# Cross-attention and a spectral feed-forward layer on one core: the rows of W are no longer folded, the first matrix sum runs for even and odd rows apart, and the first six tiles are reordered

## The chip, the cores and the metric

The kernel runs on one core of one Trainium2 chip. The metric is the time of one execution on the device in microseconds (us); lower is better. Five engines work side by side, each through its own list of instructions in order, and wait for each other by semaphores: TensorE (PE, with its weight loads shown apart as PEld), VectorE (DVE), ScalarE (ACT), GpSimd (POOL) and SyncE (SP), which here only issues transfers. PE writes to PSUM, a small memory of banks; DVE or ACT copies results from there to SBUF.

## The reference

Two blocks follow each other on x, of shape (2, 2048, 512), all in float32. The first is cross-attention with 16 heads of 32 over 128 context rows. The second is a linear layer given by its spectrum W, a complex 512 x 512 matrix.

```
x = x + attention(layernorm(x), ctx, mask)
    q = h @ wq + bq;  k = ctx @ wk + bk;  v = ctx @ wv + bv
    score = (q . k) / sqrt(32) * mask;  score = -1e9 where score == 0
    softmax(score) @ v, heads joined, @ wo + bo
x = x + real(ifft(fft(layernorm(x)) @ W)) + bias
```

The second block is linear, so the kernel computes one real 512 x 512 matrix from W and the tables of cosines and sines, and multiplies with that.

## The kernel before

The 4096 rows of x are cut into 8 groups of 512, and each group into 4 tiles of 128 rows. A tile is written (group, tile) here: (0,0), (0,1) and so on. A tile begins with its score products: `scores` (L309) makes 16 heads in two halves of eight, each half in a PSUM buffer of its own (`ps_sc`, two buffers, so one tile at a time). For each half `Softmax` does:

- `masked` (L338, DVE): product with the mask, which frees the score buffer
- `maxima` (L345, L347, L348, DVE): the marking of zeros, the smallest negated score and its scaling
- `exponentials` (L354, ACT): eight exponentials, each with its sum
- `divided` (L366 on DVE, L367 on POOL): the reciprocal of the sums and the product with it

`transposed_weights` (L384) transposes the finished weights of the tile before on PE, a PSUM bank for four heads, and copies each bank out on ACT or DVE. It runs in two halves of two banks. `context` (L406) multiplies with v when all four tiles of a group are there, `Project` makes the output product o (L204), `Ffn` the second block's product y (L204), and `Queries` the queries (L204), whose copy with the bias is on ACT (L297). Rows of x are prepared two groups ahead: `relative` (L238) subtracts the first element of each row, `query_statistics` (DVE, then rstd on POOL, L217 and L218) finds mean and deviation, `query_norm` (L221, DVE) applies them and `query_transposes` (L190, copied by ACT on L192) turns a tile.

Three PSUM pools decide what PE may start: `ps_sc`, `ps_tp` with two banks for transposes, and `ps_mm` with two banks for everything else. A product waits until the copy from the bank two products earlier has ended.

**How the matrix m_ffn is made.** W's real and imaginary parts, `wr` and `wi`, have the symmetry of rows k and 512 - k under cosine and sine. `FoldRows` (L606) uses it: a matmul with the flipped identity `flip` turns a block of rows, and DVE writes the sum and the difference of the two blocks (L625, L628), with the row 0 put in by hand (L627, L630). `fold_columns` (L636, POOL) does the same for columns and writes `cols`. Then the first sum, four `Mirrored` objects `h`, multiplies `cols` by half of the tables (`dft`, 256 rows): columns 0 to 256 by cosines, 1 to 255 by sines, two matmuls each (L689). The eviction (L697) copies the cosine half with an added first row and the sine half, and writes cosine minus sine, mirrored, and cosine plus sine. The result is `half`. The second sum, four `Mirrored` objects `m`, does the same with `half` and writes `m_ffn`. The added rows come over small transfers (`rows_h`, `rows_m`, L667) and a small transpose on PE (L673).

**What sets the order.** All instructions are placed by hand. The first five tiles, (0,0) to (1,0), are written out (L847 to L970) and hold the preparation of m_ffn between their softmax steps. From (1,1) on, `slot` (L724) lays out a tile in a fixed scheme: scores, then `pool` and `early` work, the first maximum, a first product, the first exponentials, the second mask product and so on. With its argument `soon` the first exponentials stand ahead of the first product's copy and DVE copies the first two transposed banks; the second exponentials then stand ahead of ACT's copies of the last two. Before, one tile (6,1) is laid out so. The loop at L973 calls `slot` for groups 1 to 5; tile (1,2) begins with the transposes of group 3 (L1016). The last two groups are written out again.

SP issues all loads of x, masks, weights and tables and most stores, in program order. A load into a buffer that is still read waits on that queue, and everything behind it too. `wr` and `wi` lie in the two buffers that later hold the residual rows `x_0` and `x_1`.

Of the kernel before, what the change touches and what calls it, by code (L numbers as in the profile page):

```python
# [9 lines left out]
FP = mybir.dt.float32  # L10
# [4 lines left out]
P = 128  # L15
# [7 lines left out]
def kernel(  # L23
# [76 lines left out]
    flip = const_tile([P, P], "flip")  # L100
    nc.vector.tensor_copy(flip, ident[:, P - 1 :: -1])
# [55 lines left out]

    wr = big_tile("x", 2, "wr")
    wi = big_tile("x", 2, "wi")
    row0 = const_tile([1, 2, D], "row0")  # L160
    nc.sync.dma_start(row0[:, 0, :], wf_re[0:1, :])
    nc.sync.dma_start(row0[:, 1, :], wf_im[0:1, :])
    nc.sync.dma_start(wr[:, :HC, :], chunks(wf_re[1 : HD + 1, :]))
    nc.sync.dma_start(wr[:, HC:, :], chunks(wf_re[HD:, :]))
    nc.sync.dma_start(wi[:, :HC, :], chunks(wf_im[1 : HD + 1, :]))
    nc.sync.dma_start(wi[:, HC:, :], chunks(wf_im[HD:, :]))
# [4 lines left out]
    nc.sync.dma_start(dft[:, :HC, :], chunks(dft_cos[HD:, :]))  # L171
    nc.sync.dma_start(dft[:, HC:, :], chunks(dft_sin[HD:, :]))
# [27 lines left out]
    def chain(name, lhs, rhs, width=D, between=()):  # L200

        ps = ps_mm.tile([P, D], FP, tag="mm", name=name)[:, :width]
        for c in range(NC):
            nc.tensor.matmul(  # L204
                ps, lhs(c), rhs(c), start=(c == 0), stop=(c == NC - 1)
            )
            if c == HC - 1:
                call(between)
        return ps
# [69 lines left out]
    class Queries:  # L279


        def __init__(self, i, g, first=0):
            self.i, self.g, self.first = i, g, first

        def pe(self):
            i, g = self.i, self.g
            if i not in qTs:
# [5 lines left out]
                width=GQ - self.first * P,  # L293
            )

        def evict(self):
            nc.scalar.activation(  # L297
                qTs[self.i][:, self.g, self.first * P :],
                self.ps,
                AF.Identity,  # L300
                bias=bq[:, self.g : self.g + 1],
            )
# [299 lines left out]
    m_ffn = const_tile([P, NC, D], "m_ffn")  # L602
    half = big_tile("pt", 6, "half")
    cols = big.tile([P, 4, HC, HD], FP, tag="cT", bufs=1, name="cols")

    class FoldRows:  # L606
# [3 lines left out]
        def __init__(self, name, t, other, sign, c):  # L610
            self.name, self.t, self.other, self.sign = name, t, other, sign
            self.c = c

        def pe(self):

            t, c = self.t, self.c
            self.low = ps_mm.tile([P, D], FP, tag="mm", name=f"low_{self.name}_{c}")
            nc.tensor.matmul(
                self.low, flip, t[:, HC - 1 - c, :], start=True, stop=True
            )  # L620

        def evict(self):
            t, c = self.t, self.c
            total, high = t[:, HC - 1 - c, :], t[:, HC + c, :]
            nc.vector.tensor_tensor(total, self.low, high, ALU.add)  # L625
            if c == 0:
                nc.vector.tensor_copy(total[0:1, :], high[0:1, :])  # L627
            nc.vector.tensor_tensor(high, high, self.low, ALU.subtract)  # L628
            if c == 0:
                nc.vector.tensor_scalar(  # L630
                    high[0:1, :], row0[:, self.other, :], self.sign, None, ALU.mult
                )

        on_vector = True

    def fold_columns():  # L636


        up, down = slice(HD + 1, D), slice(HD - 1, 0, -1)
        rp, rm, ip, im = wr[:, :HC, :], wr[:, HC:, :], wi[:, :HC, :], wi[:, HC:, :]  # L640
        for k, (x1, x2, op, first) in enumerate(
            (
                (rp[:, :, up], rp[:, :, down], ALU.add, rp[:, :, HD : HD + 1]),
                (im[:, :, up], im[:, :, down], ALU.add, im[:, :, HD : HD + 1]),
                (ip[:, :, down], ip[:, :, up], ALU.subtract, rp[:, :, 0:1]),
                (rm[:, :, up], rm[:, :, down], ALU.subtract, im[:, :, 0:1]),
            )
        ):
            nc.gpsimd.tensor_tensor(cols[:, k, :, 1:], x1, x2, op)
            nc.gpsimd.tensor_copy(cols[:, k, :, 0:1], first)  # L650

    def cols_of(what, g):
        return lambda i: cols[
            :,
            2 * what + i // HC,
            HC - 1 - i if i < HC else i - HC,
            g * P : (g + 1) * P,
        ]
# [11 lines left out]
    def first_rows(name, rows, scale):  # L670
# [4 lines left out]
        nc.scalar.mul(add, ps, scale)  # L675
        return add

    class Mirrored:
# [3 lines left out]
        def __init__(self, name, lhs, dst, scale):  # L682
            self.name, self.lhs, self.dst, self.scale = name, lhs, dst, scale

        def pe(self):
            ps = ps_mm.tile([P, D], FP, tag="mm", name=self.name)
            self.even, self.odd = ps[:, : HD + 1], ps[:, HD + 1 :]
            for i in range(NC):
# [3 lines left out]
                    dft[:, i, : HD + 1] if i < HC else dft[:, i, 1:HD],  # L692
# [4 lines left out]
        def evict(self, add, eng=nc.gpsimd):  # L697
            low, high = self.dst[:, 1:HD], self.dst[:, D - 1 : HD : -1]
            nc.scalar.activation(
                self.dst[:, : HD + 1],  # L700
                self.even,
                AF.Identity,
                bias=add,
                scale=self.scale,
# [117 lines left out]
    for t in range(TG):  # L822
        relative(1, t, nc.gpsimd if t < 2 else nc.vector)
    query_statistics(1, 0, TG - 1)
    for g in range(NC):
        first_queries(0, g)
# [406 lines left out]
```

## Time and profile before

| what | us |
|---|---|
| median of 3 runs | 538.68 (538.62 to 538.73) |
| profiled execution, its own time | 538.3 |
| its span, from the first to the last instruction | 536.1 |
| PE idle until the ident of POOL is there (L523) | 1.3 |
| PE idle before y, waiting for x (L507) | 0.6 |
| PE idle before the second pair of turned tiles, waiting for xnT (L192), two times | 0.5 |
| first score product, tile (0,0), starts | 20.1 |
| score product of (1,0) starts | 80.8 |
| score product of (1,2) starts | 112.0 |
| four tiles in the middle, (2,0) at 141.47 to (3,0) at 202.06 | 60.6 |

The span is some 2 us shorter than the time of the same execution. Busy time of PE counts each matmul with its latency, so neighbouring matmuls overlap in it; the distance between the starts of two products tells more than the sum of their lengths. The granted clock of TensorE was 0.999 over the span. Each matmul in float32 shows as two instructions in the trace, here called passes, each with its weight load.

### The profile page before, as it was taken

The page shows a single profiled execution, that of the slowest core. Times are in us where ns is not written, and L with a number is a line of the kernel's source. Part 1 is how long each engine was busy: PE and PEld are TensorE (multiplying, and loading weights), DVE is VectorE, ACT ScalarE, POOL GpSimd, SP SyncE. Part 2 cuts the span into 40 slices and gives each one's busy share as a digit, 9 for nine tenths or more (in the row PEclk, how much of TensorE's full clock was granted, in tenths as well). Part 3 has the DMA queues.
Part 4 walks back from the last instruction along what each step waited for, and adds up shares of the span by engine and source line. Part 5 has one row for each costly group of instructions (what it writes and reads, how often), then busy time and mean ns, then how long its engine had stood idle before and what let it go on. Part 6 is the DMA issues. An engine that isn't in the chain of part 4 may idle for free.

```text
span 536.1 us, 8773 instructions
## 1 busy us (share of the span) xinstructions
PE 525.3 (98%) x3005; PEld 293.2 (55%) x3005; DVE 439.4 (82%) x619; ACT 342.2 (64%) x1299; POOL 326.5 (61%) x266
## 2 busy tenths in 40 slices
PE   8979999999999999999999999999999999999997
PEld 7745567455545555455545555455545555455444
DVE  4698887799987998879887998879967899898351
ACT  3376786676687766666677666666776676766210
POOL 3246768935795449825795459825754466856450
PEclk9999999999999999999999999999999999999999
DMA  8960203000510005000510006000311201201102
GB/s 310 384 228 1 70 10 100 1 0 2 190 47 2 20 28 209 1 21 1 192 45 0 21 20 205 13 20 1 119 40 31 70 1 60 98 2 39 40 0 79
DMA packets 22992, 36.49 MB, mean 68 GB/s; under 512 B 2202, under 2 KB 6562, under 8 KB 22948
## 3 DMA queue, kind: packets, MB, share of 16 engines
q1 hardware_dynamic: 22260, 34.75, 18.7%
q10 hardware_dynamic: 688, 1.18, 0.6%
q8 instruction: 24, 0.39, 0.3%
q14 instruction: 20, 0.16, 0.1%
HBM read 27.53 MB, written 8.39 MB: 67 GB/s over the span
## 4 chain that ended last, share of the span: by engine, by line
PE 76%; DVE 17%; ACT 5%; POOL 1%; issue 1%; ACTq 0%; POOLq 0%; DVEq 0%
PE y L204 16%; PE o L204 16%; PE q L204 15%; PE tpw L384 8%; PE c L406 5%; PE sc L319 5%; ACT w L354 4%; DVE w L345 4%; DVE nmax L347 3%; DVE w L338 3%; PE tp_a L190 3%; PE tp_f L190 2%; PE k L551 1%; PE v L204 1%; DVE norm_f L221 1%
## 5 line engine op out<-in xcount | busy, mean ns | idle before, releaser
L354 ACT ACTIVATE w<-w,nmax 128x128 f32<-128x128 f32 x512 | 198.3, 395 | 19.6 <-DVE nmax L348 18.0
L367 POOL TENSOR_TENSOR w<-w,rden 128x1024 f32<-128x1024 f32 x62 | 119.3, 1924 | 83.4 <-DVE rden L366 67.2
L204 PE MATMUL o<-wo,cT 128*128 128x512 f32 x256 | 115.3, 594 | 0.0
L204 PE MATMUL q<-xnT,wq 128*128 128x512 f32 (+1 forms) x256 | 112.0, 582 | 2.6 <-ACT qT L297 1.5
L204 PE MATMUL y<-m_ffn,nT 128*128 128x512 f32 x248 | 112.1, 594 | 0.6 <-DVE x L507 0.6
L391 ACT COPY pt<-tpw 128x512 f32<-128x512 f32 x120 | 64.1, 587 | 56.5 <-PE tpw L384 56.4
L354 ACT ACTIVATION_READ_ACCUMULATOR w<-w,nmax 128x1 f32 x512 | 98.9, 193 | 0.0
L345 DVE SCALAR_TENSOR_TENSOR w<-w 128x1024 f32<-128x1024 f32 x64 | 88.7, 1386 | 0.9
L338 DVE TENSOR_TENSOR w<-sc,mask 128x1024 f32<-128x1024 f32 x64 | 77.4, 1211 | 12.4 <-PE sc L319 11.8
L347 DVE TENSOR_REDUCE nmax<-w 128x8 f32<-128x1024 f32 x64 | 78.1, 1220 | 2.2
L384 PEld LDWEIGHTS tpw<-ident,w 128*128 128x128 f32 x496 | 57.7, 141 | 31.8 <-issue 29.3
L204 PEld LDWEIGHTS q<-xnT,wq 128*128 128x128 f32 x256 | 46.3, 190 | 48.6 <-issue 40.2
L204 PEld LDWEIGHTS o<-wo,cT 128*128 128x128 f32 x256 | 46.2, 190 | 47.5 <-issue 46.1
L204 PEld LDWEIGHTS y<-m_ffn,nT 128*128 128x128 f32 x248 | 44.5, 190 | 45.2 <-issue 44.2
L384 PE MATMUL tpw<-ident,w 128*128 128x128 f32 x496 | 64.8, 273 | 0.7 <-POOL m_ffn L711 0.5
L462 POOL TENSOR_TENSOR x<-x,bf 128x512 f32<-128x512 f32 x32 | 50.5, 1577 | 19.0 <-DVE norm_f L221 19.0
L217 POOL TENSOR_SCALAR rstd_f<-mv_f 128x1 f32<-128x1 f32 x32 | 18.1, 564 | 65.1 <-DVE mv_f L214 65.1
L422 POOL TENSOR_TENSOR x<-x,bo 128x512 f32<-128x512 f32 x32 | 47.9, 1529 | 0.0
L238 POOL TENSOR_SCALAR rel<-rows 128x512 f32<-128x512 f32 x26 | 42.3, 1639 | 1.3 <-PE tp_a L190 1.3
L319 PEld LDWEIGHTS sc<-kT,qT 32*128 32x128 f32 x1024 | 31.5, 186 | 15.1 <-issue 12.9
L366 DVE RECIPROCAL rden<-den 128x8 f32<-128x8 f32 x64 | 12.6, 197 | 32.1 <-ACT w L354 31.9
L192 ACT COPY nT<-tp_f 128x512 f32<-128x512 f32 x29 | 16.9, 582 | 33.8 <-PE tp_f L190 33.6
(100 smaller groups left out, 552.4 us busy)
## 6 DMA issues: line engine op xcount, KB each, us to landing
rows<-in_x_dram SPq DMA_DIRECT2D x32, 256.0 KB, 5.2
x<-in_x_dram SPq DMA_DIRECT2D x32, 256.0 KB, 4.6
out_dram<-x SPq DMA_DIRECT2D x31, 256.0 KB, 2.0
mask<-in_mask_Bx1xSxS_fk_dram SPq DMA_DIRECT2D x8, 256.0 KB, 5.0
wk<-in_L_xattn_wk_w_dram ACTq DMA_DIRECT2D x2, 512.0 KB, 6.3
wq<-in_L_xattn_wq_w_dram SPq DMA_DIRECT2D x1, 1024.0 KB, 7.6
wr<-n_L_ffn_w_freq_real_dram SPq DMA_DIRECT2D x2, 512.0 KB, 5.2
wi<-n_L_ffn_w_freq_imag_dram SPq DMA_DIRECT2D x2, 512.0 KB, 7.4
```

The lines of the kernel that those rows point to most:

```text
L204: nc.tensor.matmul(ps, lhs(c), rhs(c), start=(c == 0), stop=(c == NC - 1))
L238: eng.tensor_scalar(d, xt, xt[:, 0:1], None, ALU.subtract)
L319: nc.tensor.matmul(sc[r // 2][:, r % 2, g, :], qTs[i][rows, g, t * P : (t + 1) * P], kT[rows, g, b * K : (b + 1) * K], start=True, stop=True,)
L338: nc.vector.tensor_tensor(self.w, self.sc.rearrange("p r g k -> p (r g) k"), self.mrow, ALU.mult)
L345: nc.vector.scalar_tensor_tensor(w, w, 0.0, w, ALU.is_equal, ALU.subtract)
L347: nc.vector.tensor_reduce(self.nmax, w, AX.X, ALU.min)
L354: nc.scalar.activation(w[:, h, :], w[:, h, :], AF.Exp, bias=self.nmax[:, h : h + 1], scale=-UNIT, accum_out=self.den[:, h : h + 1],)
L367: eng.tensor_tensor(w, w, rden.unsqueeze(2).to_broadcast([P, HH, K]), ALU.mult)
L384: nc.tensor.transpose(ps[:, r, :], ws[r // 2].w[:, (r % 2) * NC + g, :], ident)
L391: nc.scalar.copy(dst, ps)
L422: nc.gpsimd.tensor_tensor(xs[:, t, :], xs[:, t, :], bo, ALU.add)
L462: nc.gpsimd.tensor_tensor(xt, xt, bf, ALU.add)
```

## The change

Rows of W are not folded. `wr`, `wi` and the tables are loaded so that partition p holds rows 2p and 2p + 1 of each half of 256 rows, which puts even and odd rows into blocks of their own. Columns are still folded, on POOL: `add_columns` writes `cols`, `subtract_columns` writes in place into `wr` and `wi`. They stand early, in the start and in tile (0,0).

The first sum, now class `First`, runs over all 512 rows in eight matmuls instead of four, for even and odd rows apart. Against a table, even rows are symmetric and odd rows antisymmetric around column 128, so 129, 128, 127 and 128 columns suffice. ACT copies the bank out, scaled by 1/512; `first` on POOL makes even plus odd and even minus odd, `second` on DVE makes cosine plus sine and cosine minus sine. The weights of these matmuls are every second column of the folded W. No first row has to be added to `half`, so `rows_h`, `row0` and `flip` go. The second sum is as before but for the scale.

Two of the four remaining query products of group 0 use the banks of `ps_tp` (`spare`). In tiles (0,0) to (1,1) the order is rewritten: the value products come one tile earlier, the first sums lie in (0,1) and (0,3), m[0] moves to (1,0) and m[3] to (1,1), the queries of group 2 begin in (0,3), more transposed banks are copied by DVE, the rows of group 3 are loaded ahead of (0,2), and (1,1) is laid out with `soon`.

```diff
-    nc.sync.dma_start(row0[:, 0, :], wf_re[0:1, :])
-    nc.sync.dma_start(row0[:, 1, :], wf_im[0:1, :])
-    nc.sync.dma_start(wr[:, :HC, :], chunks(wf_re[1 : HD + 1, :]))
...
+    for to, of in ((wr, wf_re), (wi, wf_im)):
+        for rs, cs in halves_of_rows:
+            nc.sync.dma_start(to[:, cs, :], parted(of[rs, :]))
...
-    nc.sync.dma_start(dft[:, :HC, :], chunks(dft_cos[HD:, :]))
-    nc.sync.dma_start(dft[:, HC:, :], chunks(dft_sin[HD:, :]))
...
+    for rs, cs in halves_of_rows:
+        nc.sync.dma_start(cosines[:, cs, :], parted(dft_cos[rs, : HD + 1]))
+        nc.sync.dma_start(sines[:, cs, :], parted(dft_sin[rs, 1:HD]))
...
+    def add_columns(k):
+        t = (wr, wi)[k]
+        nc.gpsimd.tensor_tensor(cols[:, k, :, 1:], t[:, :, up], t[:, :, down], ALU.add)
+        nc.gpsimd.tensor_copy(cols[:, k, :, 0:1], t[:, :, HD : HD + 1])
+    def subtract_columns(k):
+        t, other = ((wr, wi), (wi, wr))[k]
+        a, b = ((up, down), (down, up))[k]
+        nc.gpsimd.tensor_tensor(t[:, :, up], t[:, :, a], t[:, :, b], ALU.subtract)
+        nc.gpsimd.tensor_copy(t[:, :, HD : HD + 1], other[:, :, 0:1])
...
+    class First:
...
+            if what == 0:
+                self.lhs = [lambda c, k=k: cols[:, k, c, g::HC] for k in range(2)]
+            else:
+                self.lhs = [lambda c, t=t: t[:, c, HD + g :: HC] for t in (wi, wr)]
...
+            for k, table, odd, n in (
+                (0, cosines, 0, QD + 1),
+                (0, cosines, 1, QD),
+                (1, sines, 0, QD - 1),
+                (1, sines, 1, QD),
+            ):
+                for b in range(2):
+                    c = b * HC + odd
+                    nc.tensor.matmul(
+                        ps[:, at : at + n],
+                        self.lhs[k](c),
+                        table[:, c, :n],
+                        start=(b == 0),
+                        stop=(b == 1),
+                    )
+                at += n
...
+            self.t = work.tile([P, D], FP, tag="parts", name=f"t_{self.name}")
+            nc.scalar.mul(self.t, self.ps, 1.0 / D)
...
+            for k, op in enumerate((ALU.add, ALU.subtract)):
+                nc.gpsimd.tensor_tensor(u[:, k, :, : QD - 1], even, odd, op)
+                nc.gpsimd.tensor_tensor(
+                    self.dst[:, k * HD : k * HD + QD + 1 : QD],
+                    t[:, : QD + 1 : QD],
+                    t[:, QD + 1 :: D - QD - 2],
+                    op,
+                )
...
+        def second(self):
+            u = self.u
+            cos, sin = u[:, :, 0, : QD - 1], u[:, :, 1, : QD - 1]
+            d = self.dst.rearrange("p (a n) -> p a n", a=2)
+            nc.vector.tensor_tensor(d[:, :, 1:QD], cos, sin, ALU.add)
+            nc.vector.tensor_tensor(d[:, ::-1, HD - 1 : QD : -1], cos, sin, ALU.subtract)
```

The new order of the six tiles, as the changed kernel has it (`w[0]` and `w[1]` are the two halves; the calls for copies name the engine where it is not ACT):

```
(start)  relative(1, 0..2); query_statistics(1, 0, 3); add_columns(0), (1); first_queries(0, g); query_transposes(0, 3)
(0,0)  w[0].masked; rest[0]; w[0].maxima; relative(1, 3, vector); query_statistics(1, 3, 4); load_rows(2); load_mask(1)
       w[0].exponentials; w[1].masked; rest[1..3]; w[1].maxima; w[1].exponentials; subtract_columns(0); query_norm(1, 0..3)
       w[0].divided; values[0].pe; w[1].divided; values[0].evict; subtract_columns(1)
(0,1)  w[0].masked; query_transposes(1, t), relative(2, t, gpsimd); w[0].maxima; values[1].pe; w[0].exponentials; w[1].masked
       values[1].evict; tpw(0,0) a; w[1].maxima; h[0].pe; w[1].exponentials; h[0].evict; w[0].divided; tpw(0,0) b, vector
       query_statistics(2, 0, 4); q[0]; w[1].divided; h[0].first; load_rows(3)
(0,2)  w[0].masked; q[1].pe; w[0].maxima; w[0].exponentials; w[1].masked; q[1].evict; tpw(0,1) a, vector; w[1].maxima
       q[2]; tpw(0,1) b; w[1].exponentials; query_norm(2, 0..3); w[0].divided; h[0].second; q[3]; w[1].divided
(0,3)  w[0].masked; h[1].pe, evict, first; w[0].maxima; h[2].pe, evict, first; w[0].exponentials; w[1].masked
       tpw(0,2) a, vector; h[1].second; h[3].pe, evict, first; query_transposes(2, 0..3); w[1].maxima; w[0].divided
       relative(3, 0); h[2].second; h[3].second; load_residual(0); rows_m; w[1].exponentials; tpw(0,2) b, vector
       q[0] of group 2; w[1].divided; relative(3, 1); load_mask(2)
(1,0)  w[0].masked; m[0].pe; add_m; m[0].evict; w[0].maxima; relative(3, 2), (3, 3); m[1].pe; w[0].exponentials; w[1].masked
       tpw(0,3) a, vector; w[1].maxima; w[0].divided; m[1].evict; m[2]; tpw(0,3) b; w[1].exponentials; query_statistics(3, 0, 2)
       q[1].pe; q[1].evict, vector; context(0, 0, 2, vector); w[1].divided; query_statistics(3, 2, 4)
(1,1)  slot with soon: context(0, 2, 4) and m[3] early, then q[2] and q[3] as its first and second product, no third
```

## Prediction

> **What bounds the kernel now.** I read the page first, for the busy shares and the slices.
>
> ```profile
> span 536.1 us, 8773 instructions
> PE 525.3 (98%) x3005; PEld 293.2 (55%) x3005; DVE 439.4 (82%) x619; ACT 342.2 (64%) x1299; POOL 326.5 (61%) x266
> ...
> PE   8979999999999999999999999999999999999997
> ```
>
> PE (TensorE) is full except in the first slices of 13.4 us: only there can a new order win time, and what PE is ahead by when the full stretch begins stays to the end. So I cut that part at the starts of the score products, one window a tile: (0,0) at 20.1 us, (0,1) at 36.4, and so on to (1,3).
>
> ```profile
> 20.10:36.40 16.30, 13.89 (x71) 7.59 (x70) 14.85 (x25) 8.99 (x38) 3.18 (x3) 1.00 0.95 344
> 36.40:50.30 13.90, 13.61 (x86) 8.01 (x85) 11.69 (x18) 9.61 (x39) 9.76 (x6) 1.00 0.01 2
> 50.30:63.90 13.60, 13.42 (x74) 7.12 (x73) 13.23 (x20) 7.77 (x27) 8.87 (x11) 1.00 0.05 5
> 63.90:80.80 16.90, 15.72 (x98) 11.66 (x98) 12.69 (x20) 14.49 (x60) 12.04 (x11) 1.00 0.19 60
> 80.80:96.80 16.00, 15.46 (x113) 10.64 (x113) 11.70 (x16) 10.73 (x38) 14.42 (x13) 1.00 0.28 83
> 96.80:112.00 15.20, 15.20 (x92) 7.53 (x88) 13.56 (x17) 11.16 (x45) 12.29 (x10) 1.00 0.00 1
> ```
>
> After the length come PE, weight loads, DVE (vector), ACT (scalar), POOL (GpSimd). Tiles (0,0) and (0,3) have the gaps, (1,1) has none, and DVE is nearly as full as PE. The waits name the gaps:
>
> ```profile
> PE q L204 <- ACT qT L297: 1.5, 1, 1.5
> PE q L204 <- ACT odd_half L709: 1.0, 1, 1.0
> PE low_wr L618 <- ACT qT L297: 0.9, 1, 0.9
> ```
>
> Each is a PSUM bank whose copy stands behind eight exponentials on ACT. Prices come from the chain in order of time, where a piece lasts until the next begins, free of the overlap in busy time:
>
> ```profile
> 36.46 1.10 PE sc L319 x32
> ...
> 47.77 0.87 PE tpw L384 x8
> 48.65 0.88 PE low_wi L618 x2
> ...
> 78.98 1.73 PE m L689 x8
> ...
> 95.03 1.85 PE c L406 x16
> ...
> 114.22 3.44 PE o L204 x8
> ```
>
> A 512-wide pass is 3.44 / 8 = 0.43 us, a flip two of them (0.86), a sum of the transform 1.73, a four-matmul chain 3.44. The o at 114.22 is the first product of tile (1,2); from there both kernels issue the same work and I compare there. From 20.1 to 114.2 the pieces add to 87.7 us; 6.4 of the 94.1 is PE waiting.
>
> **The change on PE.** Four flips go: 4 x 0.86 = 3.44. The transpose of rows_h goes: 0.20. Each first sum gets 16 passes of 127 to 129 columns for 8 of 255 to 257, the same columns. At 128 columns q_first needs 3.57 us for 32 passes, 0.112 each: 16 x 0.112 = 1.79 against 1.73, four times +0.06 = 0.24. Net PE work: -3.4 us. If all waiting went too, 9.8: the best bound.
>
> The weights of these sums are now read with a step of two elements; every weight load in the trace is contiguous. Lower bound nothing; upper bound a load of twice the 0.112, so 16 x 0.112 = 1.8 a sum and 7.2 in all. I take nothing, since 128 columns are loaded as before. [...]
>
> **The other engines.** DVE loses per W two 128x512 sums and two differences (0.66, 0.69) and two one-row operations (0.60, 0.41): 2 x 3.71 = 7.4 us, out of tiles (0,0) and (0,1). It gains four second steps of two 254-element operations, by the 255-element vector row of L710 and L711 0.41 + 0.42, 3.3 us; five pairs of bank copies that were ACT's (1.28 a pair, four of them before (1,1)); and one query copy (0.69). A vector mirror of 0.83 goes. POOL's four column folds of 1.26 become four of twice the elements, 2.5 each (bounds 2.2 by the fastest, 1.09; 3.5 with a lock of 1 us), and go to the first two tiles, where POOL is busy 3.2 and 9.8 us; they end near 25 and 41 and their readers are at 43 and 66. Their neighbours, the rstd of group 1 and the rel of group 2, slide 2 us and are read by DVE at 30 and 47. Each first step is 2 x 0.73 + 2 x 0.19 = 1.8 on POOL (L710, L650), in place of the 1.46 of a mirrored half. ACT's copy of a first sum is one of 0.69 instead of 0.48 + 0.38.
>
> On SP's queue two one-row loads and four of rows_h go. W arrives in four loads as before. The tables take four loads with rows of about 1 KB, for two with 2 KB; at worst half the 380 GB/s makes the 1 MB last 2.8 us longer. wo, issued behind them, landed at 18.4 + 13.7 = 32; tables are read at 43 and the rows of group 2 at 41, so it is hidden. The rows of group 2 now wait for the fourth rel on DVE near 26 and hold the mask behind them, not read until 80. The rows of group 3 leave some 28 us earlier, into buffers free at 47. x_0 waits for the last first sum (70) instead of leaving at 62, with rows_m behind it; POOL adds to x_0 after 98.
>
> **The order, tile by tile** (trace times; before's own value in brackets). In (0,0) the fourth rel no longer blocks DVE until 20.2, so the first mask product starts at 21.4 (23.03). rest[2] and rest[3] go into the transposing banks, idle since 20.8: the 1.5 goes, and the 0.9 with the flips. PE: 20.1 + 1.1 + 32 x 0.33 + 3.44 (v) = 35.2 (36.4). (0,1): 13.6 of work and 0.7 for the copies of xnT behind the second exponentials: 49.5 (50.3). (0,2): 13.2 and 0.3, because the weights of (0,1) are divided only after the rstd of group 2 (statistics end 50.8, 1.3 + 1.9 on POOL, 54.2): 63.0 (63.9). (0,3): 13.7 of work, but the four transposes of group 2 stand behind bank copies on DVE and then on ACT behind eight exponentials and h[3]: 2.6 lost, 79.3 (80.8). rows_m: h[3].second ends 77.6, four issues 2.4 and landing 1.7 make 81.7; PE wants it at 82.1. (1,0): 13.5, and 1.0 since q[1] needs the bank of m[1], whose copy now follows the exponentials of 84.4 to 87.5: 93.8 (96.8). (1,1): 13.3 without a gap: 107.2 (112.0).
>
> Then comes a wait that before has not. Under `soon` ACT copies the last two transposed banks after the second exponentials, and (1,2) opens with transposes into just those banks; behind them on PE stands all of (1,2). Before has such a slot once, at 411.65:
>
> ```profile
> 411.65 1.17 PE L319 MATMUL sc<-kT,qT 32*128 32x128 f32 x32
> ...
> 414.19 1.04 ACT L391 COPY pt<-tpw 128x512 f32<-128x512 f32 x2
> ```
>
> There the first bank is free at 414.19 + 0.57 = 414.8, 2.0 after the scores end at 412.75. Here: DVE starts (1,1) at 96.4 after q[1], two context copies and statistics; w0 ready at 100.4, second mask product 101.7, bank copies to 103.8 (PE makes the banks at 102.9), second maximum 106.8, q[3] copied 107.3, exponentials 3.15, first copy 0.59: 111.05. PE is at 108.3, so it waits 2.7. After two transposed tiles (1.0) o begins at 112.05 against 114.22: a lead of 2.2.
>
> **The lock between DVE and POOL** is not in this ledger. The row of L345:
>
> ```profile
> L345 DVE SCALAR_TENSOR_TENSOR w<-w x64: 1191/1220/2369, 24.3 to 490.1; 128x1024 f32<-128x1024 f32 x64
> ```
>
> Median 1.22, but 88.7 us over 64 is 1.39 on average and the worst 2.37: one wait costs up to 1.15. Between (0,2) and (1,1) the path runs through three of them: 3 x 0.17 = 0.5. I take 2.2 - 0.5 = **1.7 us faster**. Bounds: no lock 2.2; one wait of 1.2 in (0,2), where POOL's division (52.3 to 54.2) meets the first L345 at 52.3, and its echo in (0,3), 0.6. [...]
>
> The profiled execution took 538.3, of it 536.1 span; 538.3 - 1.7 = 536.6. The median of the runs is 538.68, 0.4 above; from it **537.0 us**. What this kernel can tell from no change is about 0.2%, 1.1 us.
>
> **Rivals.** *The wait in (1,2) is not there, or the gaps at (0,3) close:* PE reaches (1,2) at 107.2 and goes on, lead 4.8, 533.9. For it: PE work alone would allow 9.8. Against: the bank row above. *Gain eaten:* one to three lock waits, lead 1.1 to -1.1, 537.6 to 539.8, typically 538.1. *Slower, by a convoy:* in (0,2) to (1,1) POOL has four first steps (7.4 us) beside its divisions and rel, DVE 12 to 15 us a tile, and each L345 on the path meets a POOL instruction: four tiles x 1.15 = 4.6 against 2.2, 538.68 + 2.4 = 541.1. It decides from three full waits on. For it: POOL is busy 14.4 of 16.0 us in (1,0) already; against: the mean of 0.17 over 64 meetings. *Strided weights cost double:* 7.2 more on PE, some 2 of it inside the waits of (0,3) and (1,2): 537.0 + 5.2 = 542.2, slower too.
>
> **Chances.** Forecast 0.48 (535.5 to 537.6), no wait 0.14, eaten 0.19, convoy 0.13, double weights 0.06. Faster by over 0.2%: 0.48 + 0.14 = 0.62; within 0.19; slower 0.19. The range leaves out most of the double weights and the ends of the convoy and of the best case: 533.8 to 540.8.
>
> **What would show it.** Score starts near 35.2, 49.5, 63.0, 79.3, 93.8, 107.2; no wait on qT in (0,0); 1.8 us a first sum, 3.6 if strided loads cost double; a PE wait of 2 to 3 us for the pt copy at 108; no wait at ps_add_m. Wrong if o of group 0 begins after 114.2, if L345 in (0,2) to (1,1) averages over 1.8, or if PE waits in the shared part after (1,2).

## The result, and the profile after

| | before | after |
|---|---|---|
| median, first series (12 runs each) | 538.74 us (538.61 to 539.04) | 540.03 us (537.35 to 540.34) |
| median, second series on another chip (29 and 12 runs) | 538.47 us (538.00 to 538.91) | 537.03 us (536.52 to 539.77) |
| profiled execution, first series | 538.3 | 538.45 |
| its span | 536.1 | 536.4 |

The ratio was 1.0012 (95% interval 0.9999 to 1.0024) in the first series, which does not exclude no change, and 0.9983 (0.9973 to 0.9994) in the second. The change moves the time by less than 0.3% either way, and its sign differs between the two series. The spread says more than the medians: the runs of before lie within 1 us, those of after spread over 3 us, in groups that the granted clock tells apart. In the first series 8 of 12 runs had a mean clock of 0.996 or 0.997 and took 539.7 to 540.3 us; the other 4 had 0.999 or 1.000 and took 537.4 to 538.5.

The page of after gives the busy shares and the slices of 13.4 us. PE's busy time fell by 1.3 us (525.3 to 524.0), DVE's rose by 6.8 (439.4 to 446.2), POOL's by 10.3 (326.5 to 336.8).

```profile
span 536.4 us, 8808 instructions
...
PE 524.0 (98%) x3028; PEld 293.8 (55%) x3028; DVE 446.2 (83%) x623; ACT 336.4 (63%) x1284; POOL 336.8 (63%) x276
...
PE   8999989989999999999999999999999999999997
```

Cut at the starts of the score products, as before: length, then PE, weight loads, DVE, ACT, POOL, granted clock, DMA share, GB/s.

```profile
20.90:35.95 15.05, 15.05 (x73) 8.50 (x72) 13.25 (x16) 8.12 (x33) 8.99 (x9) 1.00 0.96 337
35.95:50.68 14.73, 14.04 (x97) 9.21 (x97) 13.45 (x21) 10.93 (x45) 14.73 (x9) 1.00 0.17 56
50.68:64.95 14.27, 13.61 (x73) 7.14 (x72) 13.62 (x20) 8.13 (x33) 7.18 (x9) 1.00 0.07 20
64.95:81.34 16.39, 14.80 (x121) 11.51 (x121) 16.22 (x21) 11.47 (x46) 12.96 (x16) 1.00 0.20 66
81.34:96.64 15.30, 14.44 (x99) 8.92 (x98) 12.84 (x19) 10.07 (x42) 12.16 (x11) 1.00 0.06 17
96.64:110.14 13.50, 13.50 (x92) 7.63 (x89) 12.64 (x19) 6.44 (x23) 11.68 (x11) 1.00 0.00 1
110.14:127.22 17.08, 14.74 (x86) 8.43 (x85) 15.78 (x18) 13.32 (x56) 8.68 (x6) 1.00 0.00 1
```

Tiles (0,0) and (1,1) are full for PE, as intended; (0,1), (0,2), (0,3) and (1,0) have gaps of 0.69, 0.66, 1.59 and 0.86 us. In (0,3) DVE is busy 16.22 of 16.39 us: it has become tighter than PE. The last row is (1,2): 2.34 us of it are PE standing still. The waits of PE name that gap first:

```profile
PE tp_a L194 <- ACT pt L398: 2.3, 1, 2.3
PE tp_a L194 <- ACT xnT L196: 1.7, 3, 1.2
...
PE q L210 <- ACT odd_m L737: 0.9, 1, 0.9
PE q L210 <- ACT qT L307: 0.7, 1, 0.7
```

In the chain the o of group 0 began at 114.80 (114.22 before). The first scores began at 20.90 (20.11), so counted from there the lead at o is 0.2 us. The timeline, which has a row begin a little earlier than the chain, puts o at 114.63 (114.05 before); all distances below go by the timeline, and the lead is the same 0.2.

### The profile page after: what moved, and what is told of

It is laid out like the page before. It is cut to its first block, busy times and chain, and to the rows that moved or that the text cites. A ratio compares the mean times of both kernels' runs of the same rounds, so it can differ in the third digit from the quotient of the medians.

```text
span 536.4 us, 8808 instructions
## 1 busy us (share of the span) xinstructions
PE 524.0 (98%) x3028; PEld 293.8 (55%) x3028; DVE 446.2 (83%) x623; ACT 336.4 (63%) x1284; POOL 336.8 (63%) x276
## 4 chain that ended last, share of the span: by engine, by line
PE 73%; DVE 19%; ACT 6%; DMA 1%; issue 1%; SPq 0%; ACTq 0%; DVEq 0%
PE y L210 16%; PE o L210 16%; PE q L210 15%; PE tpw L391 7%; PE c L413 5%; PE sc L326 5%; ACT w L361 5%; DVE w L352 5%; DVE nmax L354 4%; DVE w L345 4%; PE tp_a L194 2%; PE tp_f L194 2%; PE k L558 1%; DVE nmax L355 1%; DVE norm_f L227 1%; DMA enc<-in_ctx_dram 1%
## 5 line engine op out<-in xcount | busy, mean ns | idle before, releaser
L398 ACT COPY pt<-tpw 128x512 f32<-128x512 f32 x110 | 58.8, 586 | 56.8 <-PE tpw L391 56.6
L352 DVE SCALAR_TENSOR_TENSOR w<-w 128x1024 f32<-128x1024 f32 x64 | 89.9, 1405 | 0.8
L244 POOL TENSOR_SCALAR rel<-rows 128x512 f32<-128x512 f32 x26 | 43.6, 1689 | 1.6 <-PE tp_a L194 1.6
```

Source lines behind the costliest of these rows:

```text
L244: eng.tensor_scalar(d, xt, xt[:, 0:1], None, ALU.subtract)
L352: nc.vector.scalar_tensor_tensor(w, w, 0.0, w, ALU.is_equal, ALU.subtract)
L398: nc.scalar.copy(dst, ps)
```

## Experiments

Kernels whose labels begin with the same letter ran on one chip, beside the same runs of before. "Full clock" is a mean granted clock of 0.999 or more.

| label | edit | median | ratio to before (95%) | runs under full clock | range at full clock |
|---|---|---|---|---|---|
| a4_again | after, unchanged | 537.03 | 0.9983 (0.9973 to 0.9994) | 3 of 12 | 536.52 to 538.06 |
| a1_no_soon | no soon slot in (1,1) | 537.31 | 0.9986 (0.9978 to 0.9995) | 0 of 11 | 537.14 to 538.87 |
| a2_vec_banks | DVE copies the two banks | 536.54 | 0.9966 (0.9953 to 0.9978) | 0 of 5 | 536.52 to 538.29 |
| a3_split_folds | POOL's folds in pieces | 537.73 | 0.9983 (0.9974 to 0.9991) | 9 of 11 | 535.96 to 535.99 |
| b1_split_vec | a2 and a3 | 537.46 | 0.9971 (0.9961 to 0.9981) | 7 of 12 | 535.62 to 536.30 |
| b2_act_banks | b1, bank copies back to ACT | 536.77 | 0.9973 (0.9964 to 0.9982) | 1 of 9 | 536.57 to 537.04 |
| b3_scheme_alone | new sums, old order | 540.22 | 1.0028 (1.0013 to 1.0043) | 10 of 12 | 537.86 to 538.06 |
| b4_fill_gap | after, PE's wait filled | 537.06 | 0.9978 (0.9969 to 0.9986) | 0 of 11 | 536.59 to 538.38 |
| c1_early_norms | b1, two norms earlier | 536.48 | 0.9964 (0.9950 to 0.9977) | 0 of 5 | 536.14 to 536.69 |
| c2_fill_both | b1, its two waits filled | 535.98 | 0.9957 (0.9944 to 0.9969) | 0 of 5 | 535.77 to 536.18 |
| d1_split_fill | a3 and b4 | 536.10 | 0.9961 (0.9947 to 0.9975) | 0 of 5 | 535.94 to 536.56 |
| c3_contiguous | neighbouring weights | 537.33, one run | | 1 of 1 | |

### Where the clock goes: the wait in (1,2)

First the changed kernel once more.

> The changed kernel as it is, for comparison on this chip and for a second profile. Theory C: runs in two groups, 538.2 at clock 1.000 and 540.1 at 0.997, and a profile of the lower group shows a stretch of PEclk under 1.00 within some 5 us of the wait at 111 to 114, the rest at 1.00. Theory S: the lower group's clock is lost elsewhere, at the start or at the end.

The runs again fell into groups, lower than expected, 536.5 to 538.1 at full clock and 538.5 to 539.8 below it. This time the profiled execution was one of those with the lower clock (0.996), so its windows show the place. It is where theory C has it. The column after the five engines is the granted clock.

```profile
111.00:113.00 2.00, 0.00 (x0) 0.00 (x0) 0.95 (x3) 2.00 (x11) 0.44 (x1) 1.00 0.00 0
113.00:114.00 1.00, 0.73 (x4) 0.74 (x5) 1.00 (x1) 0.69 (x2) 0.88 (x1) 0.57 0.00 0
114.00:115.00 1.00, 1.00 (x6) 1.00 (x5) 0.97 (x2) 0.58 (x1) 1.00 (x1) 0.50 0.00 0
115.00:116.00 1.00, 1.00 (x4) 0.48 (x3) 1.00 (x1) 0.59 (x2) 0.02 (x1) 0.50 0.00 0
116.00:117.00 1.00, 1.00 (x3) 0.41 (x2) 0.97 (x2) 0.00 (x0) 0.00 (x0) 0.72 0.00 0
117.00:118.00 1.00, 1.00 (x4) 0.44 (x3) 0.97 (x3) 0.00 (x0) 0.00 (x0) 1.00 0.00 0
```

PE stands still from 110.9 to 113.27, and as it resumes its clock is halved, until 116.5; from the start to 113 and from 118 to 500 us the clock is 1.00. The four windows miss 0.43 + 0.50 + 0.50 + 0.28 = 1.71 us of full clock, and at half speed that is a stretch of 3.4 us. The distance between the two groups of runs is about that: their medians lie 1.9 us apart in the first series, 1.8 in a3 below. The profile of the first series has the same wait of 2.34 us and a clock of 1.00 throughout.

Taking the wait away in two ways:

```diff
-            soon=(i == 1),
```

in a1, and in a2

```diff
-            transposed_weights(*turned, NC // 2, NC)
+            transposed_weights(*turned, NC // 2, NC, nc.vector if soon and i == 1 else None)
```

> In tile (1,1) ACT copies the last two transposed banks ahead of the second eight exponentials, as every other slot of group 1 does, and not behind them. Theory W (the 2.3 us for which PE waits on the pt copy in (1,2) is carried to the end): that wait is gone, o of group 0 begins near 112.4 in place of 114.6 and the profiled execution takes 536.1 in place of 538.4. Theory N (PE is only stopped later, at the weights of (1,1) that come 1 us later): a wait of 1 to 2 us appears at tpw in (1,2) and the time is 537.5 to 538.4. On the runs: theory C (the wait, together with the 1.2 us at 74, lets the granted clock fall in most executions, which is why 8 of 12 runs of the changed kernel had clock 0.997 and 540.1 and 4 had 1.000 and 538.3): all runs at 0.999 or above and within 0.8 us of each other. Theory S (the two groups come from the start or from transfers): they stay, some 1.7 us apart.

> The same wait is taken away in another way: in (1,1) the last two banks are copied by DVE after its second maximum, ACT's exponentials stay where they were. DVE is free at 109.6, copies end at 110.9, PE's scores at 111.3. Theory W: o of group 0 near 112.4, 536.1 for the profiled execution. Theory N: DVE, now 1.3 us later at the next mask product, stops PE later in (1,2) or (1,3) and at most 1 us is won: 537.4 to 538.4. Theory C: all runs at clock 0.999 or above, median 536.0 to 536.5, which is 3.5 to 4 below the changed kernel's 540.0. Theory S: two groups remain, median near 537.8.

In its main point theory C held in both: 16 of 16 runs were at full clock. Its spread did not, since the runs of a1 still lie 1.7 us apart and those of a2 1.8, and the median of a2 is just above its range; the next section has the cause. Theory W did not hold. In a1 o began at 112.99, 92.57 us after the first scores and 1.2 us nearer to them than in after, but the next scores began at 127.49, no earlier than in after. A wait that after has not, in front of those scores, took the gain. The waits of PE in a1:

```profile
PE tp_f L194 <- DVE norm_f L227: 1.9, 2, 1.7
...
PE tp_a L194 <- DVE rel L227: 0.7, 1, 0.7
```

The second exponentials of (1,1) on ACT now come behind the bank copies and end at 114.3 instead of 113.1; the reciprocal of their sums stands on DVE in front of the mask product of (1,2), and the norm that PE needs before (1,3) is late with them. In a2 PE waits 0.45 and 1.41 us for DVE in the same place. So N held in what it says of the wait, which was moved and not removed, though in a1 it came at another place than N has it. Its times were missed: a1's median lies 0.2 under N's range, a2's 0.9 under it and 0.45 under the 536.99 of a4 at full clock.

The decisive kernel leaves the wait and gives PE something to do in it:

```diff
+            early=([(busy, 18)] if i == 1 else [])
+            + [(query_transposes, nn, 0), (query_transposes, nn, 1)],
```

> The changed kernel with 18 transposes of the identity into a spare bank (their result is read by nobody) on PE ahead of the xnT transposes of (1,2), about 18 x 0.11 = 2.0 us of the 2.3 us wait; every dependency and the other engines stay. Clock theory: no run under 0.999, the group near 538.4 to 540.1 is gone, and the rest is as the changed kernel's at full clock, 536.5 to 538.1. Theory S (the lower clock has nothing to do with PE standing still): 3 to 8 of 11 runs at 0.996 to 0.997 as before.

Of 11 runs none was under full clock. The chip does not explain that: beside it on the same chip b1 lost clock in 7 of 12 runs and b3 in 10 of 12. The windows of b4 over the same stretch:

```profile
111.00:112.00 1.00, 1.00 (x19) 0.88 (x12) 1.00 (x1) 1.00 (x7) 0.79 (x1) 1.00 0.00 0
112.00:113.00 1.00, 1.00 (x11) 1.00 (x10) 0.07 (x1) 1.00 (x6) 0.00 (x0) 1.00 0.00 0
113.00:114.00 1.00, 0.77 (x7) 0.53 (x6) 0.87 (x2) 1.00 (x4) 0.52 (x1) 1.00 0.00 0
```

The xnT transposes begin at 113.62, as in after (113.66), so the length of the wait is the same, and what it costs in clock is gone. That PE's standing still takes the clock, in some executions, is shown: filled waits have it in 0 of 21 runs (b4, and c2 and d1 below), the same waits left empty have it in 28 of 61 (after and a4, a3; a2, b1, b2). Why the same wait costs only some executions is not shown.

### POOL's long folds

```diff
-        nc.gpsimd.tensor_tensor(cols[:, k, :, 1:], t[:, :, up], t[:, :, down], ALU.add)
+        for c in range(NC):
+            nc.gpsimd.tensor_tensor(cols[:, k, c, 1:], t[:, c, up], t[:, c, down], ALU.add)
```

and the same in subtract_columns.

> POOL's four long column folds (2.35 and 3.15 us, 128x1020) are cut into four pieces of 128x255 each. Lock theory (a DVE operation that meets a POOL one waits for the whole POOL instruction): the first scalar_tensor_tensor of (0,0), 2.94 us beside the second column sum, falls to 1.2 to 1.9. Rival (sharing of bandwidth and no lock): it stays at 2.5 or more, since POOL moves the same elements. The time: the first score of (0,1) is set by PE's own work in (0,0), so 540.0 as the changed kernel, within 0.5, two groups of runs as there; if DVE's delay in (0,0) reaches the scores of (0,1), up to 1.2 less.

The timeline (start, duration) of the first tile, DVE's scalar_tensor_tensor beside POOL's second column sum; first of after:

```profile
22.88 2.35 POOL L620 TENSOR_TENSOR cols<-wi 128x1020 f32<-128x1020 f32 x1 [1.23 <-DMA wi<-n_L_ffn_w_freq_imag_dram]
23.36 2.94 DVE L352 SCALAR_TENSOR_TENSOR w<-w 128x1024 f32<-128x1024 f32 x1
```

and of a3:

```profile
21.10 3.78 POOL L621 TENSOR_TENSOR cols<-wi 128x255 f32<-128x255 f32 x4 [0.15 <-DMA wi<-n_L_ffn_w_freq_imag_dram]
...
22.39 1.22 DVE L352 SCALAR_TENSOR_TENSOR w<-w 128x1024 f32<-128x1024 f32 x1
```

With pieces DVE's operation takes its 1.22 (1.23 to 1.80 in the other profiles with pieces), and it is POOL that stretches, 3.78 for four pieces where the first sum's four took 2.78. In its figure the lock theory held: 2.94 fell to 1.22. That DVE waits for the whole POOL instruction is that theory's reading; the rows of after show that DVE's operation ended at 26.30, 1.07 us behind POOL's sum. The time was expected unchanged, with up to 1.2 less as the exception, and the exception came, though one tile later than expected: (0,0) stays 15.05 long, and (0,1) is 0.66 shorter. The two runs at full clock took 535.96 and 535.99, those at 0.996 took 537.6 to 538.1; a4 on the same chip has 536.5 to 538.1 and 538.5 to 539.8. Also, in a3, b1, c1, c2 and d1, with the folds in pieces, no run at full clock is above 536.7 (b2, which has pieces and other bank copies, reaches 537.0; b3 has another order); in a1, a2, a4 and b4, with whole folds, they reach 538.1 to 538.9. The upper part of after's spread at full clock goes with the long folds.

Whole folds do not always stop DVE. In c3, described below, they are whole too, but POOL's second column sum began half a us behind DVE's operation and not ahead of it:

```profile
22.51 1.22 DVE L352 SCALAR_TENSOR_TENSOR w<-w 128x1024 f32<-128x1024 f32 x1
...
23.00 2.94 POOL L620 TENSOR_TENSOR cols<-wi 128x1020 f32<-128x1020 f32 x1 [1.29 <-DMA wi<-n_L_ffn_w_freq_imag_dram]
```

There POOL's sum took 2.94 us (2.35 in after), and (0,1) took 13.97 us where after's took 14.73. In the five other profiles with whole folds (after, a1, a2, a4, b4) POOL began first, by 0.03 to 0.48 us, and DVE's operation took 2.94 to 3.40; the four of them at full clock have one of the two longest full-clock times of their kernel, 538.1 to 538.8. In these six profiles the operation that began later is the longer one, and in after, a4 and c3 POOL's sum began as `wi` landed, after waits for it of 1.23, 0.96 and 1.29 us. Such an order would divide the runs of whole folds at full clock into those near 537 and those from 538.0 on; no profile of after from the faster group is there to show it.

### Both together, and what is late next

> Both cures at once: POOL's column folds in pieces of 128x255 and DVE's copies of the last two banks in (1,1). Clock theory: all runs at 0.999 or above. Theory P (POOL's long folds delay DVE in (0,0) to (0,2) and that delay reaches PE; a3 gave 535.96 at full clock beside 536.9 to 538.1 for the changed kernel): median 535.0 to 535.9, all runs within 0.6 of each other. Rival (the folds only moved the wait): 536.5 as with the bank copies alone.

At full clock P held, with a median of 535.84 and a spread of 0.7 (535.6 to 536.3). But the clock theory failed: 7 of 12 runs lost clock again, though no single wait in (1,2) is longer than 1.41 us now. Windows of its profiled execution:

```profile
110.00:111.00 1.00, 0.03 (x1) 0.00 (x0) 1.00 (x1) 1.00 (x6) 1.00 (x1) 1.00 0.00 0
111.00:112.00 1.00, 0.56 (x3) 0.59 (x4) 1.00 (x3) 0.24 (x1) 0.46 (x2) 0.74 0.00 0
112.00:113.00 1.00, 1.00 (x4) 0.63 (x3) 0.97 (x2) 0.47 (x1) 1.00 (x1) 0.50 0.00 0
113.00:115.00 2.00, 2.00 (x4) 0.83 (x3) 1.97 (x2) 0.12 (x1) 0.44 (x1) 0.53 0.00 0
```

Waits of 0.45 and 1.41 us with 0.6 us of transposes between them did what one of 2.34 does. Filling both:

> b1 with 4 and 12 transposes of the identity on PE ahead of the two pairs of xnT transposes in (1,2), where PE waits 0.45 and 1.41; nothing else moves. In b1, 7 of 12 runs had clock 0.996 to 0.997 and took 537.4 to 538.1, the others 535.6 to 536.3. Theory (two short waits inside some 3.4 us do what one of 2.3 does): all runs at 0.999 or above, median 535.6 to 536.2. Rival (b1 loses its clock somewhere else): the two groups stay and the median is 537.4.

All five runs at full clock, 535.98: the theory held. This is the lowest median of all, 0.43% under before (0.31 to 0.56); d1, which follows, is not clearly above it. Then the version with the two edits alone, without DVE's copies:

> The changed kernel with only two edits: POOL's folds in pieces, and 18 transposes of the identity in PE's wait of (1,2); ACT still copies the last two banks of (1,1). Theory (the long folds cost 1.5 us and the spread, the clock 1.7 us in some runs, and the wait itself nothing in the end, since DVE and ACT are next): all runs at clock 0.999 or above, 535.7 to 536.2, the same as with DVE's bank copies and two fills (535.98). Rival (the 2.3 us wait is a loss of its own): 1 us or more above that, 537 or more.

It gave 536.10, within 0.2 of c2, so the theory held. In both PE still has nothing useful to do for 1.9 to 2.3 us there, so they do not show what the wait itself costs; c1, which has no such wait, does. The folds and the clock were what could be saved. One more attempt to get something for the wait:

```diff
             halves[1].masked()
+            call(norms)
             first.evict()
```

where norms are the two query_norm of (1,1) that stood in on_b; the rest as b1.

> The kernel with the folds in pieces and DVE's bank copies (b1), and in (1,1) the two norms of group 3, which stood on DVE behind the second bank copies and beside POOL's division (2.5 us for two), now stand behind the second mask product, 7 us earlier. In b1 the transposes of xnT in (1,2) wait 0.45 for the first norm and 1.41 behind the second. Theory: both waits go, o of group 0 begins 1.5 us earlier, no run under clock 0.999, median 534.2 to 535.2. Rival (the next thing late is ACT's second exponentials and with them DVE's mask product of (1,2), untouched at 111.3): the 1.4 us come back as a wait before (1,3), time 535.6 to 536.3, all at full clock.

The rival held. Both waits in (1,2) went and o began 90.19 us after the first scores (92.32 in b1's execution at the lower clock, 91.90 in c2), but PE then waited for norm_f before (1,3), as the waits of c1 say:

```profile
PE tp_f L194 <- DVE norm_f L227: 1.9, 2, 1.7
```

The scores of (1,3) began 104.86 us after the first ones, in d1 with its wait of 2.3 us 104.88: by itself the wait costs nothing. The median was 536.48, 0.2 above the upper end of what the rival had expected, at full clock in all 5 runs.

### Which half of the change pays, and who sets the pace

```diff
-    transposed_weights(0, 0, HC, NC, nc.vector)
+    transposed_weights(0, 0, HC, NC)
...
-    transposed_weights(0, 2, HC, NC, nc.vector)
+    transposed_weights(0, 2, HC, NC)
```

(four such pairs; the rest as b1)

> As the last, and four of the pairs of bank copies that the change gave to DVE ((0,1) second, (0,2) first, (0,3) both) go back to ACT, 4 x 1.28 = 5.1 us off DVE. Theory D (DVE, busy 109 to 112 of 122 us in the first eight tiles, sets the pace there and not PE): o of group 0 begins 1 to 3 us earlier than without this and the median is 533 to 534.5. Rival A (ACT's copies then stand behind eight exponentials of 3.15 us, as before the change): PE waits 1 us or more at each and the median is 536 to 538.

Theory D fell: DVE is busy for 3.5 us less than in b1 (442.7 against 446.2, where 5.1 were expected), and yet o began 92.96 us after the first scores (92.32 in b1) and the kernel took 536.6 to 537.0 at full clock, beside 535.6 to 536.3 for b1 on the same chip. Rival A is right in the time (536.77). ACT's copies behind the exponentials are what PE waits for in b2, though at two places, not at all four:

```profile
PE tp_a L194 <- ACT pt L398: 1.6, 1, 1.6
...
PE tpw L391 <- ACT pt L398: 1.2, 1, 1.2
```

So DVE's copies were a fair exchange, and DVE's load alone does not set the pace in these tiles. That the loop DVE, ACT, DVE of the softmax sets it is a reading of these waits; no run isolated it.

> The new matrix sums and column folds (in pieces) in the order of the six tiles of the kernel before: no spare banks, bank copies on ACT, no soon slot, the fourth rel before the first scores. If the scheme is the part that pays: DVE loses 7.4 us of row folds and gains 3.3, PE loses 3.4 less 0.2 to 0.9 for the sums; the lead at o of group 0 is 2 to 3 us and the median 535.5 to 536.5, clock 0.999 or above in all runs. If the order is the part that pays, or the four sums with their first and second steps in (0,3) make PE wait for m: 538 to 540.

Its edit puts before's sequence of the six tiles around First, add_columns and subtract_columns, with the folds of rows left out and the first, second and copy steps of each sum in the place of its eviction. The second branch of the expectation is the nearer one, and the median of 540.22 lies just above it. The sums alone gained little: 537.86 and 538.06 at full clock (before 538.43), and only 2 of 12 runs had it. PE has two waits as long as after's one:

```profile
PE ps_add_m L707 <- DMA rows_m<-half: 2.4, 1, 2.4
PE q L210 <- ACT qT L307: 2.0, 1, 2.0
```

The granted clock drops behind each of them (0.50 from 32 to 35 and from 83 to 86 us), a mean of 0.994. The new order takes both waits out of the way; that half of the change is worth some 2 us at full clock (b1 against the two runs of b3; b1 also has DVE's bank copies in (1,1)) and pays with the wait in (1,2).

### The step of two elements in the weights

```diff
-                self.lhs = [lambda c, k=k: cols[:, k, c, g::HC] for k in range(2)]
+                self.lhs = [lambda c, k=k: cols[:, k, c, g * P : (g + 1) * P] for k in range(2)]
```

and likewise for wi and wr.

> The first matrix sums of the changed kernel read 128 neighbouring columns as weights in place of every second one, so what they compute is another sum. If the step of two elements costs weight loads: a sum of 16 passes falls from 1.88 to 1.99 us to 1.75 to 1.8. If not: it stays at 1.88 or more, and it is the change of bank or of width that costs. The time within 0.5 of the changed kernel's either way.

The timeline of after (start, duration), a sum of 16 passes, from one start to the next group's:

```profile
68.05 1.11 PE L657 MATMUL half<-dft,wi 128*128 128x129 f32 x8
68.99 1.11 PE L657 MATMUL half<-dft,wr 128*128 128x127 f32 x8
69.93 1.04 PE L391 MATMUL tpw<-ident,w 128*128 128x128 f32 x8
```

and of c3:

```profile
66.42 1.06 PE L657 MATMUL half<-dft,wi 128*128 128x129 f32 x8
67.32 1.06 PE L657 MATMUL half<-dft,wr 128*128 128x127 f32 x8
68.21 1.04 PE L391 MATMUL tpw<-ident,w 128*128 128x128 f32 x8
```

69.93 - 68.05 = 1.88 with the step, 68.21 - 66.42 = 1.79 without. The step costs 0.09 us a sum, 0.4 for four.

## Why the prediction came out as it did

The range (533.8 to 540.8) held every run of after in both series. The forecast, 1.7 us faster and 537.0 us, did not come in the first series: the median lay 1.3 above before. In the second it came: 537.03, 1.44 faster. In part that is luck, since the median of after goes by how many executions lose clock or are held up by the folds, and the forecast priced neither in that way. The prediction's own sign of being wrong, an o behind 114.2, did come in the profile (114.80, of which 0.8 is a later start). By its own steps, tile by tile:

| length of | forecast | after | d1 (folds in pieces, wait filled) |
|---|---|---|---|
| (0,0) | 15.1 | 15.05 | 15.05 |
| (0,1) | 14.3 | 14.73 | 14.07 |
| (0,2) | 13.5 | 14.27 | 14.05 |
| (0,3) | 16.3 | 16.39 | 15.83 |
| (1,0) | 14.5 | 15.30 | 15.29 |
| (1,1) | 13.4 | 13.50 | 13.51 |
| (1,2) to o | 4.85 | 4.49 | 4.49 |

From the first scores to o that is 93.94 us before, 93.73 in after and 92.29 in d1. So with the folds in pieces the lead at o is 1.65 us, against a forecast of 1.7 with its 0.5 for DVE's meetings with POOL and 2.2 without.

- **(0,0)** was right to 0.05: no wait on qT, no flips.
- **The wait in (1,2)** was right in its place, its cause and nearly its size (2.7 forecast, 2.34 measured). What it does was not: the ledger counted it as lost length only. In some executions (20 of 35 of after, a4 and a3) the clock fell behind it, in a4 to 0.50 for some 3.4 us, a loss of 1.71 us, which the prediction has nowhere. It turned the sign: the first series' four runs at full clock lie 0.3 to 1.4 under before's median.
- **What the ledger left out is where DVE's long operation in (0,0) leads** (2.94 us beside POOL's column sum, 1.22 with the pieces). It uses up what was won at the first mask product: that starts 1.21 us after the scores (2.92 before), and the maximum behind it ends 6.86 after them (6.84 before). PE still found its banks in (0,0), which took 15.05. But the delay does not end there. With the fourth rel now inside the tile, DVE finishes the second maximum 12.8 us after the scores (11.5 before), while PE is 1.2 us earlier at the next tile. PE catches up with the softmax loop in (0,1), at ACT's copy behind the exponentials (0.40), and in (0,2) (0.66). With the folds in pieces (0,1) to (0,3) are 0.66, 0.22 and 0.56 shorter, 1.4 in all.
- **(0,3)** agrees to 0.1 by luck: PE stands still for 1.59 us where 2.6 was put, and is busy for 14.80 where 13.7 of work was put.
- **0.5 for three meetings with POOL, 0.17 each,** was too little. From (0,2) to (1,1) the eight scalar_tensor_tensors take 1.58 on average, and the worst is the one that the prediction put in its lower bound, in (0,2) at 53.15 with 2.75. Of the two operations of a second step, L689 takes 0.39 as priced, but L690 was priced 0.42 and averages 1.37, as two of the four stand beside a POOL division and take 2.1. The mean stayed under the 1.8 named as proof of the convoy, so that rival did not decide.

The two rows show it: all eight of those on DVE, with busy time and mean in ns, and the four second steps.

```profile
L352 DVE SCALAR_TENSOR_TENSOR w<-w 128x1024 f32<-128x1024 f32 x8 | 12.6, 1580 | 0.1
...
L690 DVE TENSOR_TENSOR half<-u_half 128x254 f32<-128x254 f32 x4 | 5.5, 1369 | 0.0
```

- **(1,0)**: 0.8 longer than forecast. Two of the m sums take 1.93 and 1.84 from start to start where 1.73 was put, and the wait for the m bank is 0.86 (1.0 forecast); the rest of the difference is in small pieces. No run isolated this.
- **PE's work**: first sums were put at 1.79, which is what those on wi and wr take with neighbouring weights; the step of two makes 1.88, and the second sum on cols takes 1.99 (1.89 in c3). Neither the free nor the double price was right, and 0.4 is small against 7.2. Of the 94.1 us before o the prediction took 6.4 for waiting; the windows it shows leave 4.6 idle, so by those rows the best bound was 8.0 and not 9.8.
- **"What PE is ahead by when the full stretch begins stays to the end"** is wrong for this kernel. a1 and c1 brought o forward by over 1 us against their neighbours and had it taken back before (1,3), where DVE's norm is late. Over the windows from (0,0) to (1,2) DVE is busy 97.8 of 106.3 us in after, and a lead on PE is kept only as far as DVE follows. The prediction lists DVE's terms but never adds them: 3.3 + 6.4 + 0.7 - 0.8 - 7.4 makes 2.2 us more, not less, and 6.8 were measured.
- **The start**: the first scores began 0.8 us later in the profiled execution, because the enc rows landed later (4.9 us from their issue, 4.4 before). The twelve kernels' profiles have it at 19.85 to 20.49, in no order that follows from their edits. The spread among them is not explained.

Of the rivals, "gain eaten" (537.6 to 539.8, one to three lock waits) is nearest to the runs of the first series at full clock (537.4 to 538.5), and the forecast itself (535.5 to 537.6) to those of the second: 7 of 9 lie at 536.5 to 537.1. What stays open is why the first series had 8 of 12 runs under full clock and the second 3 of 12, and why its runs at full clock lay 1 us higher; the order of POOL's column sum and DVE's operation in (0,0) would account for the second.

## What to carry to other kernels

A wait of PE is to be priced twice: by its length, which may be won back later (here the scores of (1,3) began 104.88 us after the first ones with the wait of 2.3 us and 104.86 without it), and by the clock of the stretch behind it (here 1.71 us, in 20 of 35 executions with the wait of 2.34 us left empty); where it can't be removed, it can be filled with work that nobody reads (here 0 of 21 executions lost clock). A long POOL operation in a tile where DVE is as tight as PE was worth cutting into pieces here, even at more POOL time in all: 3.78 us for the second column sum instead of 2.35, and 1.4 us less in (0,1) to (0,3). And before a lead on the fullest engine is carried to the end of a ledger, the second engine's own ledger has to be made: here DVE was 1.3 us behind at the point where PE was 1.2 us ahead.

## What was not expected of the hardware

- Waits of PE shorter than the 3.4 us of low clock behind them cost clock in some executions: 2.34 us in one piece (seen in the profiles of a4 and a3, where 3 of 12 and 9 of 11 runs were under full clock), 0.45 and 1.41 with 0.6 between (7 of 12 in b1, 1 of 9 in b2, none of 5 in a2). Single waits of 1.67 (a1, 11 runs) and 1.68 us (c1, 5 runs) cost nothing in any run. Each of the six losses in five profiles (a3, a4, b1, c3, two in b3) is 1.70 or 1.71 us by its windows, whatever the wait; b3 with waits of 2.04 and 2.41 had by its mean clock none, one or two of them. Not all of a loss need reach the end: two runs of b3 with one loss took 538.35 and 538.48, 0.3 to 0.6 above those with none. In c3 the waits of 0.54 and 1.20 at 71 to 74 us lost the clock and the 2.34 behind them did not.
- The six losses follow one pattern. Each is some 3.4 us of half clock (0.50), and in the 3.4 us ahead of it PE stands still for 1.74 (c3), 1.86 (b1), 1.9 and 2.04 (b3), 2.22 (a4) and 2.34 us (a3). What decides whether a wait costs clock no run shows: that of 2.34 us, left empty, did in 20 of 35 executions (after, a4, a3).
- Not all of DVE's operations took longer beside POOL. From 20 to 127 us of after the 14 mask products, which read PSUM and one SBUF operand, took 1.17 to 1.23 us, 1.206 on average, among them those at 51.89 and 87.12 with POOL at work; the maximum averages 1.220, as before; scalar_tensor_tensor goes to 2.94.
